# Reordering the work beside the matmuls of a two-layer graph network: inner products, mask chunks, right sums and relus

## The chip, the cores and the metric

The kernel runs on one core of a Trainium2 chip. Its metric is the device time of one execution in microseconds; lower is better. The engines of the core are TensorE (PE, with its weight loads PEld), VectorE (DVE), ScalarE (ACT), GpSimd (POOL) and SyncE (SP), which here issues all the DMAs. All data is float32.

## The reference

For each of 16 batches `x` has 1024 nodes with 512 features. Two layers follow each other; both normalize every row, apply a relu and add their result to `x`.

```python
# x (16, 1024, 512), adj (1024, 1024)
h = relu(layernorm(x))                       # layer 0
x = x + (adj @ h) @ W0 + bias
h = relu(layernorm(x))                       # layer 1
hw = h @ W1
s1, s2 = hw @ a1, hw @ a2
e = leaky_relu(s1[:, None] + s2[None, :], 0.2) * adj
x = x + elu(softmax(e, axis=2) @ hw + beta * hw)
```

## The kernel before, in words

**Products.** Every large product is done with seven block products in place of eight (the Winograd form of Strassen's scheme). Layer 0 has two per batch: the adjacency product `y = adj h`, called the A-half here, and the weight product of `y` with `W0`, the B-half. A block product is named p1 to p7 (table `PRODUCTS`, line 44). Products with the same letter (Y, W, X) accumulate in the same pair of PSUM banks, so the banks must be read between them: after p1, say, ScalarE copies bank Y to `C11`, and p6 goes on accumulating in Y.

In batch 0 the A-half runs p1 to p7 one after another (`products_a`, line 179; 14 steps). From batch 1 on (`products_a2`, line 193) four of them, p1, p5, p3 and p4, are once more split into seven *inner products* r1 to r7 of 128x256 outputs, and each inner product is interleaved with a matmul or two of a plain product: (p1, p2), (p5, p6), (p3, p7), and p4 with the first product of the B-half. That makes 28 steps k of the A-half.

In an inner split r1, r6 and r7 go one after the other into one small bank `y` (`y_p1y` and so on in the trace). r1 starts it and ScalarE copies it to `t`; r6 accumulates onto it, and VectorE adds it to the copy of r5 (`t5`); r7 accumulates again, and is read by ScalarE or VectorE, after which the sums go into the product's two banks. r7 may not start before r6 has been read, nor r6 before r1 has. For p1 the bank `i0` is complete after r7's addition, and `reads("p1", 0)` then copies it to `C11`. p6 accumulates in that bank and begins seven steps after p1.

The right-hand operands of the inner products are made once, in batch 0: `inner_right` (line 359) makes three sums `t1`, `t2`, `t4` and overwrites the block `b12` of the operand itself. `w_sums` makes the same four sums for `W0`.

**Everything else lies beside the products.** After step k, `after(k)` carries out the entries of a plan with that number; -1 is ahead of the batch's first step. Wherever an engine is called `pe`, `dve`, `act`, `pool` or `sp`, its instructions stay in the order in which the program writes them, so that the plans *are* the order of the work. SP's DMAs are in order too. The plans are dictionaries from a step to what follows it:

- `plan_out(o, b)` (line 1067) finishes batch b-1 during the A-half of batch b. `xr` tiles, four in a batch by (nh, q) with two row blocks k each, hold the residual. `keep` stores an `xr` to `x1d`; `stats` makes the sums of one row block for the second layernorm (two long and one short instruction on ScalarE with their readouts, shown as `uS<-xr`); `relu` overwrites `xr` in place with relu(layernorm), and so needs the store of `keep` to be over; `logits` multiplies by the two attention vectors (VectorE); `sums` makes the left sums of the layer-1 product and `store` puts them to DRAM; `load_res` loads the residual of batch b.
- `plan_bias` adds the bias to the residual on POOL in the first B-half steps.
- `plan_norm_a`, `plan_norm_b` normalize the next batch.
- `EARLY_B` (line 1139) does the first part of layer 1's softmax of batch 0 early, in B-halves of layer 0: `L` loads its logits, `e<g>` loads the chunk g of the mask, `M<g>` makes the masked logits (four Prelu on ScalarE, then four multiply-and-max on VectorE), `K<g>` stores the chunk to `ed`, `X` and `x` spread the maxima over DRAM, and `N n` makes the row maxima.
- `FIRST_A` and `FIRST_B` belong to the last batch of layer 0: `R<g>` reloads a chunk from `ed` (tile `er`), `E<g>` takes its exponential and transposes it, `S` and `s` sum. `load_u` loads operands of layer 1's first product (`ul_U`, `ul_S`).
- `plan_first` (line 1048) holds the sums of the right-hand operands in batch 0.

The B-half of a batch has 14 steps. `halves` of `to_residual` add each finished product bank (`po_Y`, `po_X`, `po_W`) to `xr`.

Of the kernel before, what the change touches and what calls it, by code (L numbers as in the profile page):

```python
# [61 lines left out]
def kernel(  # L62
# [130 lines left out]
    def products_a2(name, a_blk, b_blk, inner, weighted, after):  # L193


        read = ReadA(name)
        banks = {}
        by_name = {p[0]: (n, *p[1:]) for n, p in enumerate(PRODUCTS)}

        def inner_steps(prod, order=("r1", "r4", "r5", "r6", "r7", "r2", "r3")):  # L200

            _, an, bn, kind, first, last = by_name[prod]
            left, sums, right, ext = inner[prod]
            if first:
                banks[kind, 0], banks[kind, 1] = bank(f"{name}_{kind}0"), bank(f"{name}_{kind}1")
            i0, i1 = banks[kind, 0], banks[kind, 1]
            y = bank(f"{name}_{prod}y")[:, 0:256]
            x = i0[:, 256:512] if first else bank(f"{name}_{prod}x")[:, 0:256]  # L210
            t = b4.tile([P, 4, 256], F32, tag="b4", name=f"{name}_{prod}t")
            t5 = sums[:, 3].rearrange("p c d -> p (c d)")
            lefts = {
                "r1": left[:, 0:2, P : 2 * P], "r2": left[:, 2:4, P : 2 * P],
                "r7": left[:, 0:2, 0:P], "r4": left[:, 2:4, 0:P], "r5": sums[:, 0],
                "r6": sums[:, 1], "r3": sums[:, 2],
            }
            rights = {
                "r1": right[:, 0:2, 0:256], "r7": right[:, 0:2, 256:512],
                "r2": right[:, 2:4, 0:256], "r3": right[:, 2:4, 256:512],  # L220
                "r5": ext[0], "r6": ext[1], "r4": ext[2],
            }
            outs = {
                "r1": (y, True), "r4": (i0[:, 0:256], first), "r5": (x, not first),
                "r6": (y, False), "r7": (y, False), "r2": (i1[:, 0:256], first),
                "r3": (i1[:, 256:512], False),
            }

            def step(r):
                o, start = outs[r]  # L230
                for k in range(2):
                    pe.matmul(
                        o, lefts[r][:, k, :], rights[r][:, k, :], start=(start and k == 0),
                        stop=(k == 1), skip_group_check=True,
                    )
                if r == "r1":
                    act.copy(t[:, 0, :], y)
                elif r == "r5":
                    act.copy(t5, x)
                elif r == "r6":  # L240
                    add(t[:, 1, :], y, t5)
                elif r == "r7":
                    act.copy(t[:, 2, :], y)
                    if first:
                        i0v = i0.rearrange("p (a n) -> p a n", a=2)
                        add(i0v, i0v, t[:, 2:3, :].to_broadcast([P, 2, 256]))
                    else:
                        add(t[:, 3, :], y, t5)
                        add(out(0), i0, t[:, 2:4, :].rearrange("p a n -> p (a n)"))
                elif r == "r3":  # L250
                    add(out(1), i1, t[:, 0:2, :].rearrange("p a n -> p (a n)"))

            def out(p):
                return read.block("C21", p) if prod == "p4" else banks[kind, p]

            return [partial(step, r) for r in order]

        def plain_steps(prod):
            _, an, bn, kind, first, last = by_name[prod]
            if first:  # L260
                banks[kind, 0], banks[kind, 1] = bank(f"{name}_{kind}0"), bank(f"{name}_{kind}1")
            return [
                partial(
                    plain_a, banks[kind, p], p, partial(a_blk, an), partial(b_blk, bn), (k,),
                    first, last,
                )
                for p in range(2) for k in range(HC)
            ]

        def reads(prod, p):  # L270
            read(prod, p, banks[by_name[prod][3], p])

        k = 0
        for two, one in (("p1", "p2"), ("p5", "p6"), ("p3", "p7")):
            inn, pla = inner_steps(two), plain_steps(one)
            for m in range(7):
                inn[m]()
                pla[m if m < 4 else m + 1]()
                if m == 3:
                    pla[4]()  # L280
                    if one != "p2":
                        reads(one, 0)
                elif m == 4:
                    reads(two, 0)
                    if one == "p2":
                        reads(one, 0)
                elif m == 6:
                    for prod in (two, one) if one == "p2" else (one, two):
                        reads(prod, 1)
                after(k + m)  # L290
            k += 7
        inn = inner_steps("p4", ("r1", "r4", "r5", "r6", "r2", "r7", "r3"))
        steps = iter(weighted.steps(0, read.c["C11"]))
        for m in range(7):
            inn[m]()
            if m > 4:
                read.last(m - 5)
            next(steps)()
            if m == 3:
                next(steps)()  # L300
            after(k + m)
        return read.left()
# [53 lines left out]
    INNER = {"p1": ("A11", "B11"), "p5": ("S1", "T1"), "p3": ("S4", "B22"), "p4": ("A22", "T4")}  # L356
    exts = {}

    def inner_right(prod):

        r = adjT[INNER[prod][1]]
        if not exts:
# [9 lines left out]
        b11, b12, b21, b22 = (  # L372
            r[:, m : m + 2, n : n + 256] for m in (0, 2) for n in (0, 256)
        )
        add(t1, b12, b11, ALU.subtract)
        add(t2, b22, t1, ALU.subtract)
        add(b12, b22, b12, ALU.subtract)
        add(t4, b21, t2, ALU.subtract)

    inner_sums = {}  # L380

# [667 lines left out]
    def plan_first():  # L1049
        return {  # L1050
            1: [(h_sums, 0, 0), (transpose_adj, 0, 1), (transpose_adj, 1, 0), (h_sums, 0, 1)]
            + [(transpose_adj, 1, 1), (adj_sum, "T1"), (adj_sum, "T2")],
            4: [(adj_sum, "T3")], 5: [(adj_sum, "T4")], 7: [(w_sums, w0_c)],
            8: [(inner_right, "p1")], 9: [(inner_right, "p5")],
        }

    def steps(*pairs):
# [9 lines left out]
    def plan_out(o, b):  # L1067

        return steps(
            (-1, o.keep, 0, 1), (-1, o.keep, 1, 0), (-1, o.keep, 1, 1), (-1, o.stats, 0, 1, 1),  # L1070
            (0, o.stats, 1, 0, 0), (1, o.relu, 0, 0), (2, o.stats, 1, 0, 1),
            (3, o.stats, 1, 1, 0), (4, o.relu, 1, 0), (5, o.stats, 1, 1, 1), (6, o.relu, 0, 1),
            (8, o.relu, 1, 1),
            (0, inner_left, b, "p3"), (1, inner_left, b, "p4"),
            (3, o.logits, 0, 0, 0), (5, o.logits, 0, 0, 1),
            (7, o.logits, 1, 0, 0), (8, o.logits, 1, 0, 1),
            (9, o.sums, 0, 0), (10, o.sums, 0, 1), (10, o.store, 0),
            (11, o.logits, 0, 1, 0), (12, o.logits, 0, 1, 1), (12, load_res, b, 0, 0),
            (13, o.logits, 1, 1, 0), (14, o.logits, 1, 1, 1), (14, load_res, b, 1, 0),
            (15, o.sums, 1, 0), (16, o.sums, 1, 1), (16, o.store, 1),  # L1080
            (18, load_res, b, 0, 1), (20, load_res, b, 1, 1),
        )

    def plan_bias(b):
# [26 lines left out]
    def plan_softmax(order, s):  # L1111
# [25 lines left out]


    EARLY_B = {
# [3 lines left out]
    }  # L1143
    FIRST_A = {
        1: "R0", 4: "R1", 7: "B E0 R2", 9: "E1 R3", 12: "E2 R4", 14: "E3", 15: "S b", 17: "R5",
# [11 lines left out]
    for b in range(B):  # L1157
# [12 lines left out]
        else:  # L1170
            plans.append(plan_softmax(FIRST_A, sms[0]))
            plans.append({
                15: [(load_u, 0, ("U00", "U01"))], 18: [(load_u, 0, ("U10", "U11"))],
                21: [(load_u, 0, ("S2", "S1", "S4"))],
            })
            plans_b += [plan_softmax(FIRST_B, sms[0]), plan_softmax(LOGITS_B, sms[1])]
        if 0 < b <= G:
            plans.append({23: [(store_mask, b - 1)]})
        if b == 0:
            plan_b = merged(  # L1180
                {
                    1: [(inner_right, "p3")], 4: [(inner_right, "p4")], 5: [(logit_weights, 0)],
                    6: [(logit_weights, 1)],
                },
                *plans_b,
            )
            layer0_a(b, merged(plan_first(), in_fourteen(merged(*plans))))
        else:
            if b == 1:
                plans.append({-1: [(logit_weights_back, 0), (logit_weights_back, 1)]})  # L1190
            plan_b = merged(*plans_b)
            plans.append({k: plan_b.pop(i) for k, i in ((23, 0), (26, 1))})
            layer0_a2(b, merged(*plans))
# [70 lines left out]
```

## Time and profile before

| | us |
|---|---|
| median of 3 runs (2360.07 to 2361.98) | 2360.09 |
| the profiled execution | 2356.96 |
| its span, first to last instruction | 2355.2 |
| PE busy | 2300.7 (98%) |
| DVE busy | 1793.6 (76%) |
| ACT busy | 1497.9 (64%) |
| POOL busy | 601.7 (26%) |
| first matmul of batch 1 / batch 2 / layer 1, from the span's start | 97.0 / 173.2 / 1182.6 |

In the trace almost every instruction has the line of a helper, 111, so groups are told apart by their tiles: `y_*` belongs to the adjacency product, `po_*` to the weight product, `z_*` and `pq_*` to layer 1. A row "tile <- tile: us, times, longest" of the waits is an idle stretch of an engine with the instruction that ended it. A matmul of 128x512 starts 429 ns after the one before it when nothing holds it, and one of 128x256 216 ns after; more than that is a hold, or a lowered clock. In the timelines the columns are start, duration, engine, line, operation, output <- inputs, size and number of equal instructions in a row, and in brackets the idle time before it with what ended it.

### The profile page before, as it was taken

Reading aid. Unit: us, or ns where it says so; the run is one execution under the profiler, and the core shown is the slowest. Engines: PE = TensorE matmul, PEld = TensorE weight load, DVE = VectorE, ACT = ScalarE, POOL = GpSimd, SP = SyncE. Lnnn points to the kernel's source line nnn. Section 1 sums busy time; section 2 is a strip of 40 time slices with the busy share of each in tenths; the row PEclk is TensorE's granted clock in tenths of the full one; section 3 lists DMA queues with packets and bytes.
Section 4 is the critical chain, followed back from the end, with each engine's and each line's share of the span. In section 5 each row is a group of like instructions: output and inputs, shape, how many; then the busy total and the mean of one; then the engine's idle time right before and its main releaser. Section 6 shows DMA issues by size and latency. Waiting matters only on the chain.

```text
span 2355.2 us, 28469 instructions
## 1 busy us (share of the span) xinstructions
PE 2300.7 (98%) x7984; PEld 1512.2 (64%) x7984; DVE 1793.6 (76%) x3932; ACT 1497.9 (64%) x4025; POOL 601.7 (26%) x680
## 2 busy tenths in 40 slices
PE   9899999999999999999899999999999999999998
PEld 5577777777767776777655666556665566655665
DVE  4877877777787777877778778777877778777774
ACT  4456667655767666676256676766766777666743
POOL 1233233333323332233102221122211222102220
PEclk9999999999999999999899999999999999999999
DMA  6254544454454544434664455554565545555541
GB/s 228 63 185 156 168 147 131 140 170 136 161 179 136 178 161 163 164 101 142 205 208 147 160 195 198 183 176 160 197 207 184 172 160 170 185 174 172 173 131 41
DMA packets 207247, 383.15 MB, mean 163 GB/s; under 512 B 80240, under 2 KB 88432, under 8 KB 207088
## 3 DMA queue, kind: packets, MB, share of 16 engines
q1 hardware_dynamic: 206768, 380.81, 49.1%
q8 instruction: 63, 1.03, 0.2%
q14 instruction: 96, 0.79, 0.1%
q10 hardware_dynamic: 320, 0.52, 0.1%
HBM read 251.92 MB, written 133.50 MB: 164 GB/s over the span
## 4 chain that ended last, share of the span: by engine, by line
PE 60%; DVE 16%; ACT 13%; DMA 6%; issue 3%; SPq 1%; POOL 0%; ACTq 0%; DVEq 0%
PE z_Y L111 15%; PE z_X L111 7%; PE pq_Y L111 7%; PE po_Y L111 6%; PE y_Y L111 5%; DVE uS L111 5%; PE z_W L111 4%; ACT uS L111 3%; PE pq_X L111 3%; ACT xr L111 3%; PE po_X L111 2%; PE po_W L111 2%; DVE xr L111 2%; PE pq_W L111 2%; PE y_X L111 2%
## 5 line engine op out<-in xcount | busy, mean ns | idle before, releaser
L111 POOL TENSOR_TENSOR x<-x,r 128x512 f32<-128x512 f32 x120 | 226.4, 1898 | 873.5 <-DVE x L111 557.7
L111 ACT ACTIVATE e<-e,nm 128x256 f32<-128x256 f32 x480 | 237.4, 498 | 156.3 <-DVE nm L111 156.3
L111 DVE CUSTOM_DVE_ANT_0 e<-e,mask 128x256 f32<-128x256 f32 x512 | 233.2, 508 | 65.5 <-DMA mask<-maskd 30.8
L111 POOL TENSOR_TENSOR xr<-xr,bias_bc 128x512 f32<-128x512 f32 x128 | 167.2, 1329 | 244.4 <-DMA xr<-in_x_dram 156.7
L111 PE MATMUL z_Y<-pT,ul_U 128*128 128x512 f32 x512 | 224.9, 592 | 0.0
L111 ACT ACTIVATE e<-s2b,s1b 128x256 f32<-128x256 f32 x512 | 214.7, 506 | 8.6 <-DVE sz L111 8.6
L111 DVE STREAM_TRANSPOSE pT<-e 128x512 f32<-128x512 f32 x240 | 155.6, 686 | 67.9 <-ACT e L111 67.7
L111 PE MATMUL po_Y<-w_c,y_C 128*128 128x256 f32 x768 | 189.7, 381 | 2.6 <-DVE xr L111 2.6
L111 DVE CUSTOM_DVE_ANT_0 uS<-xr,v_bc 128x512 f32<-128x512 f32 x240 | 165.4, 689 | 23.4 <-ACT uS L111 15.4
L111 PE MATMUL pq_Y<-w_c,z_C 128*128 128x256 f32 x768 | 175.5, 380 | 2.1 <-DVE z L111 1.4
L111 PEld LDWEIGHTS z_Y<-pT,ul_U 128*128 128x128 f32 x512 | 97.3, 190 | 115.6 <-issue 111.5
L111 ACT ACTIVATE r<-z,rs 128x256 f32<-128x256 f32 x192 | 95.7, 499 | 110.1 <-DVE z L111 110.1
L111 PEld LDWEIGHTS pq_Y<-w_c,z_C 128*128 128x128 f32 x768 | 145.1, 190 | 32.0 <-issue 7.7
L111 PEld LDWEIGHTS po_Y<-w_c,y_C 128*128 128x128 f32 x768 | 146.3, 191 | 23.9 <-DVE xr L111 3.4
L111 PE MATMUL y_Y<-adjT_B,h 128*128 128x512 f32 (+1 forms) x332 | 153.1, 565 | 1.7 <-ACT adjT_B L111 1.7
L111 ACT ACTIVATE uS<-xr 128x512 f32<-128x512 f32 x120 | 74.9, 624 | 123.3 <-DVE xr L111 105.2
L111 PE MATMUL y_W<-adjT_B,h 128*128 128x512 f32 x256 | 129.8, 603 | 0.0
L111 PE MATMUL y_Y<-adjT_T,hS 128*128 128x512 f32 x256 | 128.0, 596 | 0.0
L111 ACT ACTIVATE h<-x,nb_h,r_h 128x512 f32<-128x512 f32 (+1 forms) x132 | 98.1, 792 | 44.1 <-POOL nb_h L111 44.1
L111 DVE TENSOR_TENSOR xr<-po_Y,xr 128x512 f32<-128x512 f32 x128 | 87.8, 687 | 43.9 <-PE po_Y L111 43.9
L111 PE MATMUL po_X<-w_c,y_S 128*128 128x256 f32 x512 | 116.3, 380 | 2.8 <-DVE xr L111 2.8
L111 ACT COPY z_C<-z_Y 128x512 f32<-128x512 f32 x96 | 55.6, 580 | 95.3 <-PE z_Y L111 95.3
(202 smaller groups left out, 4985.8 us busy)
## 6 DMA issues: line engine op xcount, KB each, us to landing
mask<-maskd SPq DMA_DIRECT2D x128, 512.0 KB
x<-in_x_dram SPq DMA_DIRECT2D x64, 512.0 KB
xr<-in_x_dram SPq DMA_DIRECT2D x256, 128.0 KB
x1d<-xr SPq DMA_DIRECT2D x64, 512.0 KB
ul_U<-ud_U SPq DMA_DIRECT2D x64, 512.0 KB
x<-x1d SPq DMA_DIRECT2D x64, 512.0 KB
out_dram<-x SPq DMA_DIRECT2D x252, 128.0 KB
ud_U<-xr SPq DMA_DIRECT2D x60, 512.0 KB
```

Source lines behind the costliest of these rows:

```text
L111: return lambda *args, **kwargs: tc.keep_in_program_order(f(*args, **kwargs))
```

## The change

Only orders change; every engine gets the instructions that it had.

1. In the inner splits of p1, p5 and p3 the order r7, r2 becomes r2, r7 (p4 had it already), and the first read of p1, p5 and p3 comes after inner product number 5, not 4.
2. `inner_right` is cut in two parts, the three new sums and the overwriting one. p1 and p5 get both parts one step earlier in batch 0's A-half, p3 and p4 get their first part in the A-half (steps 9 and 10) and their second one early in the B-half (steps 1 and 2). `w_sums` moves from step 7 to 6, `logit_weights` from 5, 6 to 3, 5.
3. The eight mask chunks were masked two in a batch, in the B-halves of batches 8 to 11; now they are masked one in a batch, in those of batches 5 to 12: load at step 4, masking at 8, store at 12.
4. In `plan_out` statistics move up and relus down: relu(0,0) from step 1 to 3, relu(1,0) from 4 to 5; logits, sums, stores and residual loads come one step later, the first two logits two.
5. In the last batch of layer 0 `load_u` moves from steps 15, 18, 21 to 22, 25 and the B-half's step 3.

```diff
-        def inner_steps(prod, order=("r1", "r4", "r5", "r6", "r7", "r2", "r3")):
+        def inner_steps(prod):
...
-            return [partial(step, r) for r in order]
+            return [partial(step, r) for r in ("r1", "r4", "r5", "r6", "r2", "r7", "r3")]
...
                     if one != "p2":
                         reads(one, 0)
-                elif m == 4:
+                elif m == 5:
                     reads(two, 0)
...
-        inn = inner_steps("p4", ("r1", "r4", "r5", "r6", "r2", "r7", "r3"))
+        inn = inner_steps("p4")
...
-    def inner_right(prod):
+    def inner_right(prod, part):
...
-        add(t1, b12, b11, ALU.subtract)
-        add(t2, b22, t1, ALU.subtract)
-        add(b12, b22, b12, ALU.subtract)
-        add(t4, b21, t2, ALU.subtract)
+        if part == 0:
+            add(t1, b12, b11, ALU.subtract)
+            add(t2, b22, t1, ALU.subtract)
+            add(t4, b21, t2, ALU.subtract)
+        else:
+            add(b12, b22, b12, ALU.subtract)
...
-            4: [(adj_sum, "T3")], 5: [(adj_sum, "T4")], 7: [(w_sums, w0_c)],
-            8: [(inner_right, "p1")], 9: [(inner_right, "p5")],
+            4: [(adj_sum, "T3")], 5: [(adj_sum, "T4")], 6: [(w_sums, w0_c)],
+            7: [(inner_right, "p1", 0), (inner_right, "p1", 1)],
+            8: [(inner_right, "p5", 0), (inner_right, "p5", 1)], 9: [(inner_right, "p3", 0)],
+            10: [(inner_right, "p4", 0)],
...
-            (0, o.stats, 1, 0, 0), (1, o.relu, 0, 0), (2, o.stats, 1, 0, 1),
-            (3, o.stats, 1, 1, 0), (4, o.relu, 1, 0), (5, o.stats, 1, 1, 1), (6, o.relu, 0, 1),
+            (0, o.stats, 1, 0, 0), (1, o.stats, 1, 0, 1), (2, o.stats, 1, 1, 0),
+            (3, o.relu, 0, 0), (4, o.stats, 1, 1, 1), (5, o.relu, 1, 0), (6, o.relu, 0, 1),
             (8, o.relu, 1, 1),
             (0, inner_left, b, "p3"), (1, inner_left, b, "p4"),
-            (3, o.logits, 0, 0, 0), (5, o.logits, 0, 0, 1),
-            (7, o.logits, 1, 0, 0), (8, o.logits, 1, 0, 1),
-            (9, o.sums, 0, 0), (10, o.sums, 0, 1), (10, o.store, 0),
-            (11, o.logits, 0, 1, 0), (12, o.logits, 0, 1, 1), (12, load_res, b, 0, 0),
-            (13, o.logits, 1, 1, 0), (14, o.logits, 1, 1, 1), (14, load_res, b, 1, 0),
-            (15, o.sums, 1, 0), (16, o.sums, 1, 1), (16, o.store, 1),
-            (18, load_res, b, 0, 1), (20, load_res, b, 1, 1),
+            (5, o.logits, 0, 0, 0), (7, o.logits, 0, 0, 1),
+            (8, o.logits, 1, 0, 0), (9, o.logits, 1, 0, 1),
+            (10, o.sums, 0, 0), (11, o.sums, 0, 1), (11, o.store, 0),
+            (12, o.logits, 0, 1, 0), (13, o.logits, 0, 1, 1), (13, load_res, b, 0, 0),
+            (14, o.logits, 1, 1, 0), (15, o.logits, 1, 1, 1), (15, load_res, b, 1, 0),
+            (16, o.sums, 1, 0), (17, o.sums, 1, 1), (17, o.store, 1),
+            (19, load_res, b, 0, 1), (21, load_res, b, 1, 1),
...
-        5: {10: "L"}, 8: {4: "e0", 8: "M0 K0 e1", 11: "M1 K1"},
-        9: {4: "e2", 8: "M2 K2 e3", 11: "M3 K3 X"}, 10: {4: "e4", 8: "M4 K4 e5", 11: "M5 K5"},
-        11: {4: "e6", 8: "M6 K6 e7", 11: "M7 K7 x"}, 13: {9: "N n"},
+        4: {10: "L"},
+        **{
+            5 + g: {4: f"e{g}", 8: f"M{g}", 12: f"K{g}" + {3: " X", 7: " x"}.get(g, "")}
+            for g in range(NCH)
+        },
+        13: {9: "N n"},
...
-                15: [(load_u, 0, ("U00", "U01"))], 18: [(load_u, 0, ("U10", "U11"))],
-                21: [(load_u, 0, ("S2", "S1", "S4"))],
+                22: [(load_u, 0, ("U00", "U01"))], 25: [(load_u, 0, ("U10", "U11"))],
...
+                steps((3, load_u, 0, ("S2", "S1", "S4"))),
...
-                    1: [(inner_right, "p3")], 4: [(inner_right, "p4")], 5: [(logit_weights, 0)],
-                    6: [(logit_weights, 1)],
+                    1: [(inner_right, "p3", 1)], 2: [(inner_right, "p4", 1)],
+                    3: [(logit_weights, 0)], 5: [(logit_weights, 1)],
```

More of the change, by code (lines that the diff above doesn't have):

```diff
@@ L1172 @@
             plans.append({
-                15: [(load_u, 0, ("U00", "U01"))], 18: [(load_u, 0, ("U10", "U11"))],
-                21: [(load_u, 0, ("S2", "S1", "S4"))],
-            })
-            plans_b += [plan_softmax(FIRST_B, sms[0]), plan_softmax(LOGITS_B, sms[1])]
+                22: [(load_u, 0, ("U00", "U01"))], 25: [(load_u, 0, ("U10", "U11"))],
+            })
+            plans_b += [
+                plan_softmax(FIRST_B, sms[0]), plan_softmax(LOGITS_B, sms[1]),
+                steps((3, load_u, 0, ("S2", "S1", "S4"))),
+            ]
         if 0 < b <= G:
```

## The prediction

> **What bounds the kernel now.** The busy table comes first: TensorE (PE) is busy 98% of 2355.2 us, so the only time that can be had is where PE stands still or is clocked down. The waits of PE say where it stands.
>
> ```profile
> engine line waited for: us in total, times, longest us
> PE y_p1y L111 <- DVE y_p1t L111: 15.3, 6, 3.9
> PE y_p4y L111 <- DVE y_p4t L111: 7.0, 1, 7.0
> PE y_p3y L111 <- DVE y_p3t L111: 5.3, 15, 1.6
> PE y_p5y L111 <- DVE y_p5t L111: 4.2, 2, 3.9
> PE po_X L111 <- DVE xr L111: 2.8, 2, 1.4
> PE po_Y L111 <- DVE xr L111: 2.6, 1, 2.6
> ```
>
> Every line that the change can touch is layer 0. `y_p1y`, `y_p3y`, `y_p5y` and `y_p4y` are the bank that inner products r1, r6 and r7 share: DVE must have read r6 before r7 may accumulate. `po_*` waits stand in the weight product of batch 0. Next, the start-to-start distance of successive matmuls against its undisturbed value (429 ns for 128x512, 216 ns for 128x256). Summed from the timeline, the excess is: batch 0's B-half 6.4 us, b1 7.3, b2 to b8 0.8 each, b9 to b12 3.0, 6.1, 3.2, 6.3, b13 0.8, b14 1.6, b15 17.8. That is 58 us in reach; a quiet batch lasts 69.75 us.
>
> Why r7 waits is read from the ScalarE (ACT) timeline of the bad batch 10:
>
> ```profile
> 739.77 0.19 ACT L111 ACTIVATION_READ_ACCUMULATOR uS<-xr,mv_u 128x1 f32 x1
> 742.75 1.52 ACT L111 ACTIVATE xr<-xr,nb_u,r_u 128x512 f32<-128x512 f32 x2 [2.80 <-DMA x1d<-xr]
> 744.18 0.35 ACT L111 COPY in_p<-y_Y 128x256 f32<-128x256 f32 x1
> ```
>
> The relu overwrites `xr` in place, so it waits 2.80 us until `x1d` has been stored. The copy of r5 (named in_p<-y_Y here, since tile names are reused) stands behind it, DVE's r6 add needs that copy, and PE's r7 needs the add. A quiet batch shows how full ACT is even without that:
>
> ```profile
> 250.43 0.20 ACT L111 ACTIVATE mv_u<-mv_u 128x1 f32<-128x1 f32 x1
> 250.66 0.72 ACT L111 ACTIVATE uS<-xr,mv_u 128x512 f32<-128x512 f32 x1
> ...
> 253.08 0.35 ACT L111 COPY y_p1t<-y_p1y 128x256 f32<-128x256 f32 x1
> 254.20 0.59 ACT L111 COPY y_C<-y_Y 128x512 f32<-128x512 f32 x1 [0.77 <-DVE y_Y L111]
> 254.68 1.52 ACT L111 ACTIVATE xr<-xr,nb_u,r_u 128x512 f32<-128x512 f32 x2
> ```
>
> Here ACT waits for DVE only 0.77 us before C11's copy, and PE needs that copy at p6's first matmul:
>
> ```profile
> 256.73 1.02 PE L111 MATMUL y_Y<-adjT_T,hS 128*128 128x512 f32 x2
> ```
>
> The copy ends at 254.79, so it is 1.9 us early. Last, the windows of batch 0's B-half, a bad batch and the last one (columns: stretch, PE, PE load, DVE, ACT, POOL busy, granted clock):
>
> ```profile
> 64.00:97.00 33.00, 27.53 (x119) 21.91 (x118) 32.52 (x52) 11.20 (x29) 12.45 (x12) 1.00 0.11 6
> 733.00:808.00 75.00, 71.11 (x273) 52.34 (x272) 56.70 (x125) 48.31 (x123) 23.03 (x33) 0.98 0.48 161
> 1096.20:1183.00 86.80, 74.30 (x274) 54.39 (x273) 63.91 (x134) 40.06 (x124) 16.49 (x21) 0.92 0.62 195
> ```
>
> In the first DVE is the bound (32.52 of 33 us); in the last the clock fell to 0.92.
>
> **What the Trainium skill says.** "TensorE: Matmul & The Clock Gate", What's actually happening: an idle window of about 3.4 us halves the clock, and it takes a busy one to come back. The trace agrees: after gaps of 3.7, 3.9 and 7.0 us the 256-wide matmuls go at about 430 ns instead of 216 for some time (1.7 to 2.9 us lost), after gaps of 1.4 to 2.6 us none. So a long wait costs nearly its length plus 2 to 3 us. The table at the head of that page calls ScalarE's and VectorE's queues strict FIFO; the r5 copy held behind the relu agrees. "SBUF — State Buffer", SBUF: two separate sides: a VectorE operation with two SBUF inputs and a GpSimd operation that reads SBUF exclude each other for a whole instruction. The trace agrees: inner right sums take 0.69 us alone, and 1.64 to 1.79 beside POOL's bias adds at 72 to 83 us; adds that read PSUM are not stretched.
>
> **The change part by part.** On every engine the same instructions run; only their orders change, so nothing is gained in work. Times below are relative to the batch's first r1 matmul; the ACT pitches are 1.70 us for one set of row statistics (such as 250.66's group and its first half), 1.42 for a relu pair, 0.25 (end 0.35) for a 256-wide copy.
>
> *Swap r2 before r7 (p1, p5, p3).* r7 comes one 256-wide pair with its companions later, 1.72 us. In b2 to b8 r6's add ends some 0.5 us late at p3 and 0.1 at p5, so these holds go: p1's read of r6 then has 1.8 us left, p5's 0.7, p3's 2.8. The first read of p1, p5 and p3 moves by one pair with it, and frees nothing that anyone waits for. r7's own copy and C11's copy shift with it.
>
> *Relus two steps on.* The relu of (0,0) moves from step 1 to 3, 3.4 us, past two statistics. The waits for `x1d` were at most 3.0 us, so they go. But the statistics now stand before r7's copy: one more than before. Summing ACT from its first statistics (-3.98), C11's copy ends at 13.52, against p6's need at 13.77: slack 0.2. Likewise r1's copy of p5 now follows relu (0,1), and that follows a DVE addition behind two logits: it ends at 18.48 against r6 at 18.08, a hold of 0.46 + 0.10 of restart in every batch. So quiet b2 to b5 pay 0.56 each (before 0.79): gain 1.0.
>
> *The rest of the output plan.* Logits, sums and stores come one or two pairs (1.7 or 3.4 us) later. DVE, busy 53.8 of a quiet batch's 69.75 us, idles 0.9 to 2.3 us in several places of the A-half's end, which hides them. The residual loads go 1.7 us later to SP and POOL's bias adds with them; DVE idles 1.03 to 1.11 us before each residual add that follows. I take 0; if the cover fails, 0.1 to 0.6 us in a batch would stand at the start of the B-half.
>
> *One mask per weight product.* Before, batches 8 to 11 masked two chunks each; the first at step 8 puts four DVE operations (0.345 each) ahead of the residual add, and ACT begins at -2.60 instead of -3.98 in the batch that follows (b9 to b12). Now batches 5 to 12 do one each at step 8: the same 1.38 falls on b6 to b13. C11's copy then ends at 14.90: a hold of 1.19 + 0.10, with p5's 0.56 and some 0.1 makes 1.94. b6 to b8: before 2.4, after 5.8, loss 3.4. b9 to b12: before 18.7, after 7.8, gain 10.9. b13: loss 1.1. b14 (top-of-row reductions push it 0.74): gain 0.3. On SP one store of 512 KB now stands where two stood, so store queues get shorter; bound 0 to 0.
>
> *b1.* Statistics come about 2.0 us late after batch 0's crowded DVE. Before: 7.3, with a 2.6 us wait for `x1d`. After: r6 0.44, C11 1.47, p5 0.65, sum 2.6: gain 4.7, from 2.3 (the relu still waits) to 6.6.
>
> *Inner sums in the first adjacency product.* Twelve DVE sums of 0.6 pitch leave the stretch where POOL's bias adds stretch six of them by about 1 us each. But in the A-half DVE also starts late (52.7) and runs without a gap, so the two reads of C22 come later: the add that ended at 58.24 ends at about 60.9, and p4 wants the bank at 59.41: a new wait of 1.5. In the B-half, holds of 0.5 to 5.6 us stay, according to how many logit weights now meet the bias adds; before 6.4. Net gain 1.5, between -0.7 and 4.4.
>
> *The last batch.* Loads of U (1 MB) leave the place ahead of the er reload that p4 waits for (7.0 us, and 2.9 of slow clock). The reload lands 3 to 4 us earlier, less what the store behind sums(1,1) loses; p4 then waits about 4.8 + 2.9. p5 3.4 + 0.9 (before 4.1 + 1.8), p3 1.3 (before 1.85), rest 0.6. 13.9 against 17.8: gain 3.9, between 0 and 9. The U loads come later, yet land well before layer 1 reads the sums 13.7 us into it.
>
> Sum: 1.5 + 4.7 + 1.0 - 3.4 + 10.9 - 1.1 + 0.3 + 3.9 = 17.8 us. The profiled execution took 2356.96; the changed one should take 2339.2. The median of the runs is 3.1 above the profile: 2342.
>
> **The rivals.**
> *All holds vanish.* If ACT finishes C11's and p5's copy some 1.3 us sooner than summed (the 0.2 us slack is the difference of long sums), the 19 us of new holds (4 x 0.56 + 8 x 1.94 + 1.3) aren't there: 2342 - 19 = 2323. For it: those two copies cost little themselves, and ACT idles 0.77 before one. Against: ACT's pitches are steady to 0.05.
> *Only the middle works.* If batch 0 loses 0.7, the last gains nothing and b1 2.3: 17.8 - 2.2 - 3.9 - 2.4 = 9.3, so 2351; with the first two alone about 2347. For it: both are chains with other late members.
> *It does not do what it says.* If a relu still waits for `x1d` after two steps, b9 to b12 keep their 18.7 and the gain is 7: 2353. Against: 3.4 us exceed the longest wait.
> *Slower.* The hold of C11's copy at p6 grows. It falls on 14 batches, so each microsecond that ACT is later than I summed costs 14 us; from 1.3 us more per batch the change loses, and at 2 us (one more statistics in front) it ends at 2342 + 28 = 2370. For it: ACT has no idle time left before that copy; against: the count of statistics is certain.
>
> **How the numbers follow.** Chances: forecast 0.58, all vanish 0.14, only the middle 0.14, not as said 0.07, slower 0.07. The forecast is 2342. The range 2326 to 2353 leaves out most of the second and the last case, and holds the unknown bounds of b0, b1 and b15 together (-9, +10). This kernel's measurement tells 0.2%, 4.7 us, from no change: faster 0.89, same 0.06 (parts of the last two cases), slower 0.05.
>
> **What would show it.** In the waits of PE, `y_p1y` and `y_p3y` for DVE are gone but for the last batch; a wait of `y_Y` for ACT's `y_C` (about 1 us, some 9 times) and of `y_p5y` for ACT's `y_p5t` (0.3 to 0.5 us, some 14 times) are new; ACT's wait for `x1d` is gone; `y_p4y` falls from 7.0 to about 5; batch 0's p4 waits 1.5 us for DVE. Wrong would be: `y_Y` waits of over 2 us in the middle batches, or a new wait on a DMA.

## The result, and the profile after

The median went from 2360.07 to 2346.45 us (five runs each, the changed ones from 2345.13 to 2351.9); the ratio is 0.9947, with a 95% interval of 0.9933 to 0.9962. That is 13.6 us faster, against the 18 us that were forecast. The profiled execution of the changed kernel took 2345.13 us, with a span of 2343.3; from profile to profile the gain is 11.8 us.

The waits of PE in the changed kernel (columns: engine and tile, what released it: us in total, times, longest):

```profile
PE y_Y L111 <- ACT y_C L111: 9.8, 9, 1.2
PE y_p4y L111 <- DVE y_p4t L111: 6.4, 1, 6.4
PE y_p5y L111 <- ACT y_p5t L111: 5.9, 15, 0.4
PE po_Y L111 <- DVE xr L111: 4.2, 2, 3.8
...
PE y_p5y L111 <- DVE y_p5t L111: 3.1, 1, 3.1
PE y_Y L111 <- DVE y_C L111: 1.4, 1, 1.4
PE y_p3y L111 <- DVE y_p3t L111: 0.8, 1, 0.8
```

The 15.3 us at `y_p1y` are gone, and so is every wait of p3 and p5 for DVE except in the last batch. Two rows are new and come batch after batch: p6 waits for ScalarE's copy to C11 (`y_Y` for `y_C`), in the nine batches b6 to b14 and about 1.1 us each, and p5's r6 waits for ScalarE's copy of r1, 15 times 0.4 us. No wait of ScalarE for `x1d` is left, where there were five, 9.0 us together.

The windows of batch 0's B-half, of batch 10 and of the last batch in the changed kernel (columns as in the prediction):

```profile
64.00:97.00 33.00, 28.76 (x114) 22.87 (x113) 32.48 (x53) 12.84 (x33) 12.59 (x12) 0.90 0.14 11
730.80:801.84 71.04, 69.49 (x274) 51.51 (x272) 54.42 (x117) 46.53 (x119) 21.92 (x33) 1.00 0.46 156
1085.30:1170.00 84.70, 73.97 (x274) 53.96 (x274) 64.32 (x134) 40.13 (x124) 15.07 (x21) 0.94 0.62 207
```

Batch 10 now takes 71.04 us, at full clock. Batch 0's B-half is no better: VectorE is busy 32.48 of 33 us as before, and PE's clock has now fallen there to 0.90.

The table adds up, for each stretch, how much later each matmul starts after the one before it than the undisturbed distance (429 ns for 128x512, 216 for 128x256, 109 for 128x128). b0 is batch 0 with the start of the kernel, b1 the first batch after it, and so on. Each row is a single profiled execution; the experiments' names are explained below.

| excess in us | b0 | b1 | b2-5 | b6-8, b13 | b9-12 | b14 | b15 | layer 0 | layer 1 |
|---|---|---|---|---|---|---|---|---|---|
| before | 12.9 | 7.3 | 3.3 | 3.3 | 18.7 | 1.6 | 17.8 | 64.9 | 6.8 |
| changed | 14.4 | 0.6 | 2.9 | 8.5 | 8.5 | 1.5 | 15.6 | 52.0 | 8.0 |
| swap_only | 12.5 | 6.1 | 4.1 | 4.3 | 16.9 | 1.8 | 16.3 | 62.0 | 11.1 |
| masks_only | 12.0 | 6.7 | 3.3 | 8.8 | 8.8 | 1.6 | 15.5 | 56.7 | 6.2 |
| no_swap | 15.6 | 0.5 | 2.5 | 7.8 | 7.8 | 1.5 | 13.3 | 49.1 | 10.3 |
| old_out | 13.3 | 3.7 | 4.1 | 9.6 | 9.8 | 1.8 | 13.7 | 56.0 | 11.2 |
| old_sums | 12.2 | 3.5 | 2.9 | 8.5 | 8.6 | 1.5 | 15.9 | 53.1 | 2.1 |
| old_loads | 14.6 | 1.5 | 2.9 | 8.5 | 8.5 | 1.5 | 17.9 | 55.4 | 12.9 |
| stat5 | 13.8 | 0.3 | 0.1 | 2.8 | 2.9 | 0.1 | 14.1 | 34.1 | 6.4 |
| relu7 | 14.1 | 0.9 | 0.6 | 6.1 | 6.2 | 0.8 | 15.8 | 44.6 | 5.4 |
| weights_late | 7.8 | 6.3 | 2.9 | 8.5 | 8.5 | 1.5 | 15.5 | 51.0 | 10.3 |
| tail_late | 13.7 | 1.6 | 3.1 | 8.5 | 8.5 | 1.5 | 12.9 | 49.6 | 7.6 |
| combo | 13.8 | 4.1 | 0.1 | 0.7 | 0.3 | 0.0 | 12.4 | 31.4 | 9.7 |
| best | 13.8 | 0.0 | 0.1 | 0.4 | 0.4 | 0.0 | 13.3 | 28.0 | 4.2 |

The middle batches repeat to 0.2 us each where their orders are the same. Batch 0, batch 15 and above all layer 1 do not: layer 1, whose orders no edit touches, has anything from 2.1 to 12.9 us. This is probably much of why one kernel's runs lie 5 us and more apart, which one profile for each kernel can't show; it is why the small differences below are read from this table and not from the medians.

### The profile page after: what moved, and what is told of

Read it like the earlier page. It is cut to its first block, busy times and chain, and to the rows that moved or that the text cites. A ratio compares the mean times of both kernels' runs of the same rounds, so it can differ in the third digit from the quotient of the medians.

```text
span 2343.3 us, 28480 instructions
## 1 busy us (share of the span) xinstructions
PE 2294.7 (98%) x7984; PEld 1511.0 (64%) x7984; DVE 1782.8 (76%) x3932; ACT 1496.8 (64%) x4025; POOL 582.9 (25%) x680
## 4 chain that ended last, share of the span: by engine, by line
PE 60%; ACT 14%; DVE 13%; DMA 7%; issue 4%; SPq 2%; POOL 0%; ACTq 0%; DVEq 0%; POOLq 0%
PE z_Y L111 12%; PE y_Y L111 9%; PE pq_Y L111 6%; PE z_X L111 6%; PE po_Y L111 6%; ACT uS L111 5%; PE z_W L111 4%; PE pq_X L111 3%; PE y_X L111 3%; DVE e L111 2%; PE po_X L111 2%; DMA md<-mx 2%; ACT e L111 2%; PE po_W L111 2%; DVE hS L111 2%
## 5 line engine op out<-in xcount | busy, mean ns | idle before, releaser
L111 ACT ACTIVATE h<-x,nb_h,r_h 128x512 f32<-128x512 f32 (+1 forms) x132 | 98.2, 793 | 44.6 <-POOL nb_h L111 43.4
```

Of the source, the lines that this page charges most:

```text
L111: return lambda *args, **kwargs: tc.keep_in_program_order(f(*args, **kwargs))
```

## The experiments

The medians of the kernel before in the four sets of runs were 2359.42, 2356.66, 2362.63 and, for the last experiment, 2356.7 us, so ratios are compared, not microseconds. The changed kernel's ratio to compare with is 0.9947.

**Each part alone, or taken out**

*swap_only*, the kernel before with part 1.

```diff
-        def inner_steps(prod, order=("r1", "r4", "r5", "r6", "r7", "r2", "r3")):
+        def inner_steps(prod, order=("r1", "r4", "r5", "r6", "r2", "r7", "r3")):
...
-                elif m == 4:
+                elif m == 5:
                     reads(two, 0)
```

> The kernel before with part 1 alone (r2 ahead of r7, first read one step later). If the holds of r7 are shortened by exactly the 1.72 us that r7 comes later, and nothing else is late next: b2 to b8 and b13 gain 0.8 each (6.3), b9 to b12 gain 1.72 each, their 0.34 at p3 and some 3 us of slow clock (11.2), b1 3.8, b14 1.2, b15 5.2; together about 27 us, median 2333. p1's waits for DVE keep 0.3 to 2.4 us in b1 and b9 to b12. Rival: C11's copy becomes late too because r7's copy shifts (a y_Y wait for ACT's y_C of about 1 us in most batches): about 2345.

Measured: ratio 0.9991 (0.9984 to 0.9998), some 2 us. The expectation of 27 us was far off, and the waits of PE name the reason, the rival's and one more:

```profile
PE y_p1y L111 <- DVE y_p1t L111: 7.2, 5, 2.4
...
PE y_p5y L111 <- ACT y_p5t L111: 6.0, 15, 0.4
PE y_Y L111 <- ACT y_C L111: 3.8, 6, 1.0
```

p1's waits for DVE halve as expected. But the swap moves r7 itself one step later in the program, and with it r7's copy on ScalarE: it now stands behind an entry of the plan that it used to precede. ScalarE's timeline of a quiet batch with the swap alone, read from the top:

```profile
322.39 1.52 ACT L111 ACTIVATE xr<-xr,nb_u,r_u 128x512 f32<-128x512 f32 x2 [0.62 <-POOL nb_u L111]
323.81 0.35 ACT L111 COPY y_p1t<-y_p1y 128x256 f32<-128x256 f32 x1
324.92 0.58 ACT L111 COPY y_C<-y_Y 128x512 f32<-128x512 f32 x1 [0.76 <-DVE y_Y L111]
```

Before, r7's copy came ahead of that relu (253.08 ahead of 254.68 in the prediction's excerpt). Now it follows it at 323.81, which is 12.26 us after the batch's first r1 in place of 10.12, and C11's copy ends at 13.96 in place of 11.83, past p6's need at 13.77. Of these 2.14 us the relu's own pitch is 1.42, and 0.62 is its wait for POOL. What r7 gained at its start, its reader lost. In b2 to b5 the swap alone makes things worse (4.1 against 3.3).

*masks_only*, the kernel before with part 3 (the lines of `EARLY_B` as in the change).

> The kernel before with part 3 alone (one mask chunk in each of batches 5 to 12). If ACT's late start of 1.38 us is what remains, r7 of p1 waits about 1.85 us and p3 0.34 in each of b6 to b13: 17.5 against 21.9 before in the same batches, so a gain of 4 us, median 2356, with no wait of a relu for x1d above 0.5 us. Rival: the store of the chunk at step 12 still holds SP ahead of the x1d stores, relus wait 2 to 3 us in eight batches rather than two: loss of 10 to 20 us, 2370 to 2380.

Measured: 0.9973 (0.9962 to 0.9984). The forecast of 4 us was right (2354.85 against 2359.42); the table shows the trade: b9 to b12 fall from 18.7 to 8.8, b6 to b8 and b13 rise from 3.3 to 8.8. That the sum came out was partly luck: in b6 p1's r7 waits 0.80 us, not 1.85, and a wait of 0.27 at p5, which was not foreseen, comes beside p3's 0.30. ScalarE's waits for `x1d` fall from five to one:

```profile
ACT xr L111 <- DMA x1d<-xr: 1.9, 1, 1.9
```

So even with the relus where they were, one chunk a batch keeps SP's queue short enough; the one row that is left is not in a mask batch but in b1.

*no_swap*, the changed kernel with part 1 undone (r7 ahead of r2 again in p1, p5 and p3, first read at step 4).

> The changed kernel with part 1 undone (r7 ahead of r2 in p1, p5 and p3, first read one step earlier), all else as changed. If the swap's own cost is that r7's copy moves behind one more entry of the plan, C11's and p5's holds go, and r7 itself waits again for VectorE's r6 read: about 0.1 us at p1 in quiet batches and 1.3 in b6 to b13, 0.35 to 0.5 at p3. Excess about 0.8 in b2 to b5 and 1.8 in b6 to b13, in place of 0.73 and 2.11: within 3 us of the changed kernel, 2344 to 2346. Rival: the swap is what makes the new plan pay, r7 waits 1.7 us and more in every batch without it: 2360 or slower.

Measured: 0.9921 (0.9905 to 0.9938), not slower than the changed kernel's 0.9947; the median of 2344.38 us lies in the expected range, though the kernel before was 2.6 us slower in this set than on record. p1's r7 waits again for VectorE in nine batches, but C11's and p5's rows are gone:

```profile
PE y_p1y L111 <- DVE y_p1t L111: 10.9, 9, 1.4
```

In b6 to b13 the excess is about 1.93 a batch without the swap and 2.11 with it, in b2 to b5 0.63 against 0.73. In this plan the swap brings nothing.

*old_out*, the changed kernel with part 4 undone.

> The changed kernel with the old order of the output plan (relu at step 1, statistics and logits as before). If the reordered plan is what makes C11's and p5's copies late, the waits y_Y for y_C and y_p5y for y_p5t go, and b1 to b14 lose only 0.1 to 0.3 us each in place of 0.56 or 1.94: gain of about 20 us on the changed kernel, median 2326. Rival: without the two steps the relu waits for x1d again in the eight mask batches (2 to 3 us), and p1's r7 waits again: about 2346 or slower.

Measured: 0.9942 (0.992 to 0.9964), no difference from the changed kernel. My expectation missed by 20 us, for the same reason as with swap_only: I had blamed the new plan for the two late copies, but with the old plan and the swap they are as late. The new plan puts one more set of statistics ahead of r7's copy; in the old one the relu of step 4 stands there:

```profile
PE y_Y L111 <- ACT y_C L111: 14.2, 10, 1.6
PE y_p5y L111 <- ACT y_p5t L111: 6.0, 15, 0.4
```

The new plan is worth 0.3 us in each of b2 to b14 and 3.1 us in b1, where the relu still waited 2.1 us for `x1d` with the old one. The 0.3 us fit a wait that only the old plan has: its relu stands 0.62 us for POOL's `nb_u` in 14 batches, and r7's copy begins at 12.26 after the batch's first r1 in place of 11.95.

*old_sums*, the changed kernel with part 2 undone (`inner_right` in one piece, entries as before).

> The changed kernel with part 2 undone (inner right sums and logit weights where they were). Batch 0 goes back from about 8 us of holds and slow clock to 6.4, p4's 1.4 us wait gone, but batch 1 begins with ACT 2 us late and pays about 2.6 us in place of 0.5: no change within 2 us of the changed kernel, about 2346. Rival: the hold of 3.8 us in batch 0's B-half and the slow clock behind it are what the moved sums cost, with nothing given back in b1: 2340.

Measured: 0.993 (0.9907 to 0.9953), which can't be told from the changed kernel. Batch 0 has 12.2 us of excess in place of 14.4, b1 3.5 in place of 0.6: what the moved sums cost in batch 0, they give back in b1.

*old_loads*, the changed kernel with part 5 undone.

> The changed kernel with part 5 undone (load_u at steps 15, 18 and 21 of the last batch). If the 1 MB of U loads ahead of the er reload is what lengthened p4's wait, it is 8 to 9 us in place of 6.4 and batch 15 has 17.5 to 18.5 us of excess in place of 15.6: 2 to 3 us slower than the changed kernel, 2349. Rival: the reload is late because it is issued late, behind the store that waits for VectorE's sums, and the loads make no difference: 15 to 16 us of excess, 2346.

Measured: 0.9946 (0.9931 to 0.9961), no difference in the time. In the last batch alone p4 waits 7.7 us in place of 6.4 and the excess is 17.9 in place of 15.6, near what the first theory had; layer 1 happened to have 12.9 in this profile. Of the 2.3 us 1.2 are p4's wait; the rest is less than the lowered clock adds by chance (behind the same wait of 3.06 us at p5 it cost 1.6 us in the changed kernel and 3.0 here). The reload is issued 51.1 us after the batch's start in place of 49.6, and takes 5.75 us in place of 5.5. But it is issued as late in no_swap (51.1) and tail_late (51.3), where the loads stand behind it. So this points to the loads at most and doesn't settle it.

Taken together: without part 1, 2, 4 or 5 alone the time can't be told from the changed kernel's, and part 3 alone is worth half of the change (0.9973). What that leaves is above all the first batch after batch 0, which needs parts 2 and 4 at once: it has 0.6 us of excess with both and 3.5 or 3.7 with one of them.

**Are the two late copies the remaining cost?**

*stat5*: one number.

```diff
-            (3, o.relu, 0, 0), (4, o.stats, 1, 1, 1), (5, o.relu, 1, 0), (6, o.relu, 0, 1),
+            (3, o.relu, 0, 0), (5, o.stats, 1, 1, 1), (5, o.relu, 1, 0), (6, o.relu, 0, 1),
```

> The changed kernel with one entry moved: statistics (1,1,1) from step 4 to step 5, so that r7's copy and C11's copy of p1 stand before them on ScalarE. If C11's hold is the statistics in front of r7's copy, C11's copy ends 1.7 us earlier (11.95 us after the batch's first r1 in quiet batches, 13.34 in b6 to b13, against a need at 13.77): the 9 waits of y_Y for y_C go, b6 to b13 fall from 2.11 us of excess to about 0.75 and b14 from 1.47 to 0.75, p5's 0.4 us waits stay. Gain 11.5 us on the changed kernel, median 2335. Rival: ScalarE is simply full at that place, the work only moves, and p5's copy waits 1.3 us longer in the same batches: no gain, 2346.

Measured: 0.9881 (0.9865 to 0.9897), more than was expected. First ScalarE in batch 6 of the changed kernel, with the statistics ahead of r7's copy, and PE's wait behind it:

```profile
458.30 0.61 ACT L111 ACTIVATE uS<-xr 128x512 f32<-128x512 f32 x1
...
460.00 0.35 ACT L111 COPY y_p1t<-y_p1y 128x256 f32<-128x256 f32 x1
461.11 0.58 ACT L111 COPY y_C<-y_Y 128x512 f32<-128x512 f32 x1 [0.77 <-DVE y_Y L111]
```

```profile
461.75 1.12 PE L111 MATMUL y_Y<-adjT_T,hS 128*128 128x512 f32 x2 [1.16 <-ACT y_C L111]
```

Then ScalarE in batch 6 of stat5, where the same statistics follow:

```profile
454.53 0.35 ACT L111 COPY y_p1t<-y_p1y 128x256 f32<-128x256 f32 x1
455.64 0.59 ACT L111 COPY y_C<-y_Y 128x512 f32<-128x512 f32 x1 [0.76 <-DVE y_Y L111]
456.12 0.63 ACT L111 ACTIVATE uS<-xr 128x512 f32<-128x512 f32 x1
```

The batch begins at 442.88 here, so C11's copy ends at 13.35, 0.4 us before p6 needs it (13.77); in the changed kernel it ended at 15.04. No wait of `y_Y` for `y_C` is left. The rival, that the work would only be late one place further on, is wrong: the statistics fill the idle time that ScalarE had before the second C11 copy (1.30 us before the one at 464.41 in the changed kernel). So p5's copy comes 1.1 us earlier in b2 to b5, and its hold vanishes there too, which I hadn't expected; in b6 to b13, where ScalarE begins 1.38 us later, p5 still waits 0.4 us.

*relu7*: the other number.

```diff
-            (3, o.relu, 0, 0), (4, o.stats, 1, 1, 1), (5, o.relu, 1, 0), (6, o.relu, 0, 1),
+            (3, o.relu, 0, 0), (4, o.stats, 1, 1, 1), (5, o.relu, 1, 0), (7, o.relu, 0, 1),
```

> The changed kernel with relu (0,1) moved from step 6 to step 7, behind r1's copy of p5 on ScalarE. If that relu is what makes the copy late, the 15 waits of y_p5y for ACT's y_p5t go and each batch loses 0.5 us less: gain 7.5 to 8.4 us, median 2338; y_Y's waits for y_C stay. Rival: p5's r7 is held instead because the relu now stands in front of r5's copy (a y_p5y wait for DVE's y_p5t in each batch): no gain, 2346.

Measured: 0.9911 (0.9896 to 0.9926), about the size that was expected. All 15 waits of p5's r6 for ScalarE are gone, C11's stay (ten of them here, 10.8 us). So C11's hold does not depend on this relu. The other way round the two are not wholly separate: stat5 took p5's hold in b2 to b5 as well.

**Batch 0 and batch 15**

*weights_late*: logit weights of batch 0 after the bias adds.

```diff
-                    3: [(logit_weights, 0)], 5: [(logit_weights, 1)],
+                    8: [(logit_weights, 0)], 9: [(logit_weights, 1)],
```

> The changed kernel with the logit weights of batch 0 at B-half steps 8 and 9 in place of 3 and 5. If they cause batch 0's 3.8 us wait of po_Y (four of them stretched to 1.63 us beside POOL's bias adds, ahead of the residual add), that wait and 2.4 us of slow clock go: batch 0's B-half falls from 7.4 us of excess to 1 or 2, and b1 stays below 1: gain about 5.5 us, median 2341. Rival: VectorE is full through the whole half, so the wait only comes at a later bank or in b1's start: gain under 2 us.

Measured: 0.9948 (0.9933 to 0.9963), no difference from the changed kernel: the rival. VectorE in the changed kernel's batch 0, with POOL's bias adds beside it until 84.2, and the matmul that waits:

```profile
79.83 1.63 DVE L111 CUSTOM_DVE_ANT_0 junk<-w_t,v_bc 128x512 f32<-128x512 f32 x1
...
83.16 1.62 DVE L111 CUSTOM_DVE_ANT_0 junk<-w_t,v_bc 128x512 f32<-128x512 f32 x1
...
84.72 1.28 DVE L111 TENSOR_TENSOR xr<-po_Y,xr 128x512 f32<-128x512 f32 x2
```

```profile
85.45 2.07 PE L111 MATMUL po_Y<-w_c,y_C 128*128 128x256 f32 x4 [3.80 <-DVE xr L111]
```

With the weights later they take 0.69 us, that wait and the slow clock behind it are gone, and batch 0 falls from 14.4 to 7.8. But VectorE works through the weights shortly before batch 1, and p1's r5 waits for its left sums:

```profile
97.57 1.13 PE L111 MATMUL y_Y<-ext,in_p 128*128 128x256 f32 x4 [2.04 <-DVE in_p L111]
```

That is one of four holds in b1, which rises from 0.6 to 6.3. The two batches together have 14.1 us in place of 15.0, so the wait has mostly changed its place. VectorE is not simply full here: in this half it stands 2.0 us for POOL's adds and PE's products before it comes to the weights. Whether a finer placing of the weights would use that time was not tried.

*tail_late*: two exponentials of the last batch.

```diff
-        1: "R0", 4: "R1", 7: "B E0 R2", 9: "E1 R3", 12: "E2 R4", 14: "E3", 15: "S b", 17: "R5",
+        1: "R0", 4: "R1", 7: "B E0 R2", 9: "R3", 11: "E1", 12: "E2 R4", 14: "E3", 15: "S b", 17: "R5",
...
-        0: "E5", 1: "D R7", 2: "E6", 4: "E7 s", 7: "T1a", 8: "T1b", 10: "d", 11: "T2a",
+        1: "D R7", 2: "E5 E6", 4: "E7 s", 7: "T1a", 8: "T1b", 10: "d", 11: "T2a",
```

> The changed kernel with two exponentials of the last batch later: E1 from step 9 to 11, E5 from the step amid p4 to step 2 of the B-half. If p4's 6.4 us wait is ScalarE standing at E5 for the reload of er with p4's copies behind it, and p5's 3.1 us wait is VectorE standing behind E1's transposes, both go with their slow clock: batch 15 falls from 15.6 us of excess to 3 or 4, gain about 11 us, median 2335. Rival: p4's copies then wait for E4 or for the next reload (R6) instead: gain under 5 us.

Measured: 0.9946 (0.9926 to 0.9965), no difference. In the changed kernel ScalarE stands at E5 for the reload:

```profile
1140.44 0.51 ACT L111 ACTIVATE er<-er,nm 128x256 f32<-128x256 f32 x1 [5.71 <-DMA er<-ed]
```

What stands behind it is not p4's copy on ScalarE, which the expectation named and which ended at 1134.73, but VectorE: it waits for E5 to transpose it, and p4's r6 read comes after that.

```profile
1142.55 1.30 DVE L111 STREAM_TRANSPOSE pT<-er 128x512 f32<-128x512 f32 x2 [4.43 <-ACT er L111]
1143.78 0.38 DVE L111 TENSOR_TENSOR y_p4t<-y_p4y,in_p 128x256 f32<-128x256 f32 x1
```

```profile
1144.22 2.07 PE L111 MATMUL y_p4y<-adjT_T,h 128*128 128x256 f32 x4 [6.44 <-DVE y_p4t L111]
```

With E5 later p4's wait is gone, as was expected, but others came in its place:

```profile
PE y_p3y L111 <- DVE y_p3t L111: 2.6, 1, 2.6
PE y_p5y L111 <- DVE y_p5t L111: 1.9, 1, 1.9
```

The wait at p3 had been 0.8, that at p5 3.1. A third wait of `po_Y` (2.38 us, at 1158.81) and two of about 1 us for ScalarE are new too. Batch 15 falls only from 15.6 to 12.9: neither theory had its size; the first had E5 right as the cause of p4's wait, but not the way from it to PE.

**A version that is faster than both**

*combo* puts stat5, relu7, E5's move and one half of the late weights (step 9) together.

> The changed kernel with statistics (1,1,1) at step 5 and relu (0,1) at step 7, E5 of the last batch at B-half step 2, and the second half of batch 0's logit weights at step 9 (the first stays at 3). If the holds are separate and sum up: b2 to b14 fall to 0.2 us of excess or less each, batch 0's B-half to about 2 with 2 to 3 in b1, batch 15 to about 9 (p4's wait gone, 2.5 at po_Y in its place): layer 0 at 23 us in place of 52, median 2317. Rival: with both entries moved, ScalarE's queue in b6 to b13 is late somewhere else (p5's r7 or p3), at 0.5 us a batch, and batch 15 keeps 13: median 2326.

Measured: 0.9837 (0.9821 to 0.9853). b2 to b14 add up to 1.1 us, so the rival's place for a new hold is wrong. Of the rest the forecast was too hopeful, and layer 0 has 31.4 us, not 23: batch 0's 3.8 us wait stayed although half of the weights had left, b1 paid 4.1, b15 fell to 12.4 and not to 9.

*best* is combo without the late weights, that is, the changed kernel with three edits:

```diff
-            (3, o.relu, 0, 0), (4, o.stats, 1, 1, 1), (5, o.relu, 1, 0), (6, o.relu, 0, 1),
+            (3, o.relu, 0, 0), (5, o.stats, 1, 1, 1), (5, o.relu, 1, 0), (7, o.relu, 0, 1),
...
-        0: "E5", 1: "D R7", 2: "E6", 4: "E7 s", 7: "T1a", 8: "T1b", 10: "d", 11: "T2a",
+        1: "D R7", 2: "E5 E6", 4: "E7 s", 7: "T1a", 8: "T1b", 10: "d", 11: "T2a",
```

> The changed kernel with statistics (1,1,1) at step 5, relu (0,1) at step 7 and E5 of the last batch at B-half step 2; batch 0's logit weights stay as the change has them (steps 3 and 5). If the 3.9 us that b1 lost with half of the weights later was VectorE's lateness alone, b1 returns to 0.3 with batch 0's B-half at 6.3 to 7.4, b2 to b14 stay at 0.1 to 0.3 and b15 at 12.4: layer 0 has 27 to 28 us of excess in place of 52, ratio to the kernel before about 0.983 (2322). Rival: b1's holds come from the two moved entries, and b1 keeps 3 to 4 us: 0.985, as with the weights later.

Measured: 0.9842 (0.9825 to 0.986), a median of 2319.16 us (2317.55 to 2322.19) beside 2356.7 of the kernel before; in time it can't be told from combo. b1 has 0.0 again, and the place of the weights is all that differs from combo, so combo's holds in b1 came from them. Layer 0 has 28.0 us of excess in place of 64.9, and nearly all that is left of PE's waits lies in batch 0 and batch 15:

```profile
PE po_Y L111 <- DVE xr L111: 7.3, 3, 3.8
PE y_p5y L111 <- DVE y_p5t L111: 2.7, 1, 2.7
PE y_Y L111 <- DVE y_C L111: 1.4, 1, 1.4
```

The other rows are of 1.4 us and less.

## Why the prediction came out as it did

The direction and most steps were right, and the measured median lies 4.5 us from the forecast, inside the range. The profiled execution missed by more, 2345.13 against 2339.2: the prediction added 3.1 us from profile to median, and for the changed kernel that step was 1.3. Both new waits that the prediction named stand in the profile. Its steps against the excess table:

- *C11's and p5's holds.* Forecast 1.29 and 0.56 us in b6 to b13; measured 1.42 and 0.66 (1.32 and 0.56 at the waiting matmul and 0.10 at the next). C11's copy ended at 13.65 in quiet batches, 0.13 later than summed, so the 0.2 us of slack were mostly used up. stat5 and relu7 show that both causes are the ones named, one set of statistics and one relu. But the prediction put the number of statistics and relus in front down to the reordered plan; old_out and swap_only show that the swap with the old plan, where a relu stands in front in place of those statistics, has them too. In the sum this made no difference, as swap and plan come together; it did in what I expected of the experiments.
- *Masks.* Forecast: b9 to b12 gain 10.9, b6 to b8 lose 3.4, b13 loses 1.1. Measured: 10.2, and 5.2 lost in the other four together. masks_only shows nearly the same figures with nothing else changed (9.9 and 5.5), though there the waits are those of r7 for VectorE. Net this step gives 5.0 us, less than the first batch after batch 0.
- *The first batch after batch 0.* Forecast 4.7, measured 6.7. The term was too small, though it went beyond the 6.6 us of its range only by 0.1: ScalarE was taken to begin 2.0 us late, but it began at -4.08, on time. no_swap keeps this gain (0.5), while old_sums (3.5) and old_out (3.7) each lose about 3 us of it: it takes the earlier end of VectorE's work and the relu's two steps.
- *Batch 0.* Forecast a gain of 1.5, measured a loss of 1.5, outside the range that the prediction gave this term (-0.7 to 4.4). The wait of p4 came as worked out (1.38 us against 1.5). The step that failed is the B-half, which should have kept 0.5 to 5.6 us and has 7.4. The count behind it was wrong: not twelve sums leave the stretch of the bias adds but six, of eight that stood there, and of those that stay one is stretched again (1.80 us). And four of the weights moved in and were stretched from 0.69 to between 1.31 and 1.63 us ahead of a residual add. The Trainium skill's statement in "SBUF — State Buffer", SBUF: two separate sides, that a VectorE operation with two SBUF inputs and a GpSimd operation that reads SBUF exclude each other, holds for them as it does for the sums. The wait of 3.80 us then also cost 2.7 us at half clock, which agrees with the idle window of about 3.4 us in the Trainium skill's "TensorE: Matmul & The Clock Gate", What's actually happening. The prediction knew both effects and named the weights as the open point, but its 5.6 us did not cover their meeting. One us of the loss is luck of the clock: nine profiles have this wait of 3.8 us, and in seven of them the slow clock cost 1.5 to 1.8 us and the B-half has 6.2 to 6.5. That is still no gain on the 6.4 of before. On the other side the start of the kernel, which no part touches, happened to have 0.9 us less.
- *Batch 15.* Forecast 3.9, measured 2.2. p4 waited 6.4 us, not 4.8. The reload landed 5.5 us after its issue (1134.96 to 1140.44), where it took 8.5 before (1144.44 to 1152.91), so it came 3 us sooner after its issue; but it was issued 1.3 us later counted from the batch's start (49.6 against 48.3). The prediction put such a gain down to the U loads. old_loads does not bear that out: with these loads ahead of it again the reload took 5.75 us. What made it take 8.5 before stays open.
- *No waits for x1d*, as forecast. masks_only shows that in the middle batches the shorter SP queue alone would have sufficed; the two steps are needed in b1.

Layer 1 adds 1.2 us to the changed kernel's profile (8.0 against 6.8). No run ties this to the change, and layer 1's own spread is larger.

The first rival, that all holds vanish, did not come true for this change, but it names what was left to gain: moving two entries of ScalarE's order took the holds of b2 to b14 from 21.4 us to 0.9 (best). The case that only the middle works was near in its two outer terms: batch 0 lost and the last batch gained little. (Its sum for these two alone, 2347, should be 2348.)

## What to carry to other kernels

Where a hand-written plan interleaves small operations with matmuls, moving a matmul to a later step also moves the copy that reads it past the entries of the plan between the two places. Before such a swap, list for each engine what newly stands in front of every copy that PE waits for. Then look for the engine's own idle gap (here 1.30 us before the second C11 copy) and put the displaced work there; in layer 0 that took off 17.9 us (52.0 to 34.1), more than the five parts of the change together (64.9 to 52.0).

When an engine is busy nearly throughout a stretch, as VectorE in batch 0, moving its operations can merely choose who waits: with the weights later, b0 fell by 6.6 us and b1 rose by 5.7. Spreading a burst over more batches (the masks) pays as long as all the shares together cost less than the burst. Here a share cost 1.4 us in each batch only because the copies behind it had no slack; in best, where they have some, it costs 0.1.

## What the runs showed of the hardware

- In layer 1, whose orders are the same in all these kernels, the excess differs by 11 us between profiled executions (2.1 to 12.9). In the changed kernel's profile its only row among PE's waits is `pq_W` for ScalarE's z_C; 7 us ahead of the one at 1439.7, ScalarE had stood 6.63 us for VectorE's row maxima, and these had stood 1.53 us for a small DMA (`mall` from `md`). That such waits make the spread was not tested.
- A gap of PE of 3.80 us cost 2.7 us at half clock (128x256 matmuls 427 ns apart in place of 216), one of 3.06 cost 1.6 (and 3.0 in old_loads), one of 2.65 in combo some 0.1 and one of 2.63, later in the same run, some 1.8 all the same. In swap_only gaps of 2.36 and 2.34 us (b10 and b12) were each followed by 1.8 us of it. So the prediction's reading, no loss after gaps of 1.4 to 2.6 us, does not hold in general, and here the measurement differs from the idle window of about 3.4 us named above: gaps shorter than it were followed by half clock. The length of a gap alone does not tell whether the clock falls.
